# Where layer 1's results lie before they are stored: first five images in place, runs of eight rows from the sixth on

## The chip, the core and the metric

The kernel runs on one core of one Trainium2 chip. The metric is device time in microseconds for one launch; three runs of the kernel before took 1414.7 to 1417.7 us, with a median of 1415.74 us. A smaller time is better.

## What is computed

The input `x` holds 16 images of 128 channels and 64 x 64 pixels in float32. Two layers are applied, each with a residual:

```
x = x + L0(groupnorm(x))     # diagonal LSTM: a scan over 64 + 63 skewed columns
x = x + L1(groupnorm(x))     # per pixel: 128 channels -> 4 angles -> 4-qubit circuit -> 128 channels
```

Layer 1 works on each pixel alone. With the normalisation folded into its weights, it is for each pixel: angles (a product with 4 rows of weights, expanded to 128 rows of signed sums), a sine, a product to amplitudes, a square, a product back to 128 channels, a bias, and the residual. Groups of four channels share their mean and variance over an image, so layer 1 can only start once layer 0 has finished every row of every image.

## The kernel before

**Where the data lies.** A tile called `ring` holds 40 of the 64 rows of all 16 images in on-chip memory, as `[128 channels, 10 blocks, 16 images, 256]`; a block is four rows of one image, 1 KB per channel, and the blocks of one image are 16 KB apart. The other 24 rows, the "low" rows, go out to a scratch tensor `low` in device memory while layer 0 runs, and must be loaded again for layer 1.

**Layer 1's tiling.** A chunk is eight rows of one image: 512 values, 2 KB, for each of the 128 channels. An image has eight chunks, k = 0 to 7. Chunks 0 to 2 are low rows (`NT` is 3); chunks 3 to 7 lie in the ring, as two neighbouring blocks, so in two pieces of 1 KB. For each image `angles` (L977) makes the angles of all eight chunks, `sines` (L992 to L997) reduces them and takes the sine, `squares` (L1006, L1019) the amplitudes and their squares, `outputs` (L1028) the products for half of the chunks, h = 0 or 1, four PSUM banks at a time out of five, and `finish` (L1053, L1054) adds bias and residual on VectorE and has SP store each chunk to `out`. Image 0 is done in two half-width passes (c = 0 and 1); the others in one (c is None).

**Where results go.** `finish` writes the result of a low chunk where the chunk was (`v`). For images 1 to 15 the result of a ring chunk goes somewhere else: for an odd image b to `ring[:, q, b-1:b+1]`, for an even one to `ring[:, q+1, b-2:b]`. These are blocks of the image itself and its neighbours that are dead by then, and as images are neighbours in memory, the 512 values are one run of 2 KB. Image 0 is written in place.

**Places for low rows.** There are 48 low chunks. `lows` lists where each of them lies, in the order of images. The first 14 places are the eight `spare` tiles and six `low` tiles; the first eight are filled during layer 0, by SP. Each `finish` appends the places that it has used to the list `places`, in order, and `load(n)` takes up to n of them from its front and has POOL load the next low chunks into them (L860). A load must wait until the store that reads its place has landed. In image 0 only the low chunks' places are appended (`c == 1 and k < NT`); from image 1 on all eight.

**What sets the order.** The stage is written under a manual schedule: each engine and queue runs its instructions in the order of the program and waits on semaphores only. In layer 1 SP's queue holds nothing but the stores, POOL's nothing but the loads. VectorE runs, for image b, four additions, the rounding of image b + 2 (L994, L995), and four more additions. The loop over b calls `outputs`, `finish(b, 0)`, `load(3)`, the sine, `squares(b + 1)`, `outputs`, `finish(b, 1)`, `load(3)`, `angles(b + 3)`.

Of the kernel before, what the change touches and what calls it, by code (L numbers as in the profile page):

```python
# [25 lines left out]
BLOCK = ROWS * NW  # L26
# [54 lines left out]
def kernel(  # L81
# [16 lines left out]
    nc = tc.nc  # L98
# [12 lines left out]
    NT = NLOW * NW // CHUNK  # L111
# [23 lines left out]
    def block(r):  # L135

        return (r + AHEAD if r < SLOTS else r - SLOTS) // ROWS
# [18 lines left out]
    with ExitStack() as scan:  # L156
# [58 lines left out]
        with ExitStack() as prep:  # L215
# [47 lines left out]
            for i in range(2):  # L263
                nc.scalar.dma_start(out=ws_n[i], in_=ws_v[:, 2 * i : 2 * i + 2])
            nc.scalar.dma_start(
                out=qw, in_=q_weights.rearrange("l w a -> (l w a)").partition_broadcast(P)
# [88 lines left out]
            for i in range(2):  # L355
                v = ws_n[i]
# [500 lines left out]
        def low_rows(queue, n, v):  # L857
            b, k = n // NT, n % NT
            of = low[b, :, k * CHUNK : (k + 1) * CHUNK]
            queue.dma_start(out=v, in_=of if len(v.shape) == 2 else of.rearrange("p (k n) -> p k n", n=BLOCK))  # L860
# [4 lines left out]
        with tc.manual_schedule():  # L865
# [26 lines left out]
            v = ring[:, block(NH - ROWS)].rearrange("p i (r w) -> p i r w", w=NW)[:, :, :, NW - STRIP :]  # L892
# [4 lines left out]
            for i, u in enumerate((d, sq)):  # L897
                u = u.rearrange("p i r w -> p i (r w)")
# [43 lines left out]

    places = list(spare) + [lowp.tile([P, CHUNK], F32, name=f"low{i}") for i in range(6)]
    lows = []

    def load(n):

        while n and places and len(lows) < NT * NB:  # L950
            v = places.pop(0)
            lows.append(v)
            if len(lows) > 8:
                low_rows(nc.gpsimd, len(lows) - 1, v)
            n -= 1

    def rows_of(b, k):
        if k < NT:
            return lows[NT * b + k]
        q = block(2 * ROWS * k)  # L960
        return ring[:, q : q + 2, b, :]

    def half(v, c):

        if c is None:
            return v
        return v[:, c] if len(v.shape) == 3 else v[:, c * BLOCK : (c + 1) * BLOCK]

    def bank(pool, name):
        return pool.tile([P, CHUNK], F32, name=name, tag=pool.name)  # L970

    def angles(b, c=None, all_of=None):
        th = half(bank(ps_t, f"theta{b}_{c}") if all_of is None else all_of, c)
        for h in range(2):

            for j in (2, 3, 1, 0):
                nc.tensor.matmul(  # L977
                    th[32 * j : 32 * j + 32, :],
                    lhsT=w_image[:, b, 16 - 16 * h : 48 - 16 * h],
                    rhs=half(rows_of(b, 2 * j + h), c),  # L980
                    start=(h == 0),
                    stop=(h == 1),
                    tile_position=(0, 32 * j),
                )
        ths[b, c] = th

    def sines(b, c=None):

        if b not in turns:
            turns[b] = sinp.tile([P, CHUNK], F32, name=f"y{b}", tag="y")  # L990
        y = half(turns[b], c)
        nc.scalar.activation(y, ths[b, c], AF.Identity, bias=b_image[:, b : b + 1])  # L992
        near = half(nearp.tile([P, CHUNK], F32, name=f"near{b}_{c}", tag="near"), c)
        nc.vector.tensor_scalar(near, y, ROUND, ROUND, ALU.add, ALU.subtract)  # L994
        nc.vector.tensor_sub(y, y, near)  # L995
        yield
        nc.scalar.activation(y, y, AF.Sin, scale=TWO_PI)  # L997

    def squares(b, c=None):
        ams = []  # L1000
        y = half(turns[b], c)
        for h in range(2):
            am = half(ps_a.tile([P, CHUNK], F32, name=f"am{b}_{h}_{c}", tag=f"am{h}"), c)

            k = 64 * h
            nc.tensor.matmul(  # L1006
                am,
                lhsT=w_amp[k : k + 64, h, :],
                rhs=y[k : k + 64, :],
                start=True,  # L1010
                stop=True,
                tile_position=(k, 0),
            )
            ams.append(am)

        if b not in sqs:
            sqs[b] = [sqp.tile([P, CHUNK], F32, name=f"sq{b}", tag="sq"), turns[b]]
        for am, v in zip(ams, sqs[b]):
            nc.scalar.activation(half(v, c), am, AF.Square)  # L1019

    def outputs(b, h, c=None):
        po = [
            half(bank(ps_o, f"po{b}_{h}_{j}_{c}"), c)
            for j in range(4)
        ]
        for j in range(4):
            k = 32 * j
            nc.tensor.matmul(  # L1028
                po[j],
                lhsT=w_out[k : k + 32, :],  # L1030
                rhs=half(sqs[b][h], c)[k : k + 32, :],
                start=True,
                stop=True,
                tile_position=(k, 0),
            )
        return po

    def finish(b, h, po, c=None):
        for j in range(4):
            k = 4 * h + j  # L1040
            v = rows_of(b, k)
            x1, y, o = half(v, c), po[j], ov[b, :, k * CHUNK : (k + 1) * CHUNK]
            to = place = v
            if c is not None:
                o, to = o[:, c * BLOCK : (c + 1) * BLOCK], x1
            elif k >= NT:


                q = block(2 * ROWS * k)
                to = ring[:, q, b - 1 : b + 1, :] if b % 2 else ring[:, q + 1, b - 2 : b, :]  # L1050
                y = y.rearrange("p (k n) -> p k n", n=BLOCK)
                place = to.rearrange("p k n -> p (k n)")
            nc.vector.scalar_tensor_tensor(to, y, b_out, x1, ALU.add, ALU.add)  # L1053
            nc.sync.dma_start(out=o, in_=to if c is not None else place)  # L1054
            if c is None or c == 1 and k < NT:
                places.append(place)

    def idle():

        ps = bank(ps_t, nc.get_next_instruction_name())  # L1060
        v = w_image.rearrange("p b k -> p (b k)")[:, 0:CHUNK]
        for _ in range(2):
            nc.tensor.matmul(ps, lhsT=w_out, rhs=v, start=True, stop=True)  # L1063

    with tc.manual_schedule():
        load(len(places))

        angles(0, 0)
        angles(0, 1, bank(ps_o, "theta0"))
        first = [sines(0, c) for c in range(2)]  # L1070
        for later in first:
            next(later)

        th = bank(ps_t, "theta1")
        angles(1, 0, th)
        for later in first:
            next(later, None)
        squares(0, 0)
        angles(1, 1, th)
        ths[1, None] = th  # L1080
        po = outputs(0, 0, 0)
        finish(0, 0, po, 0)
        squares(0, 1)
        later = sines(1)
        next(later)
        po = outputs(0, 1, 0)
        finish(0, 1, po, 0)
        next(later, None)
        po = outputs(0, 0, 1)
        finish(0, 0, po, 1)  # L1090
        load(3)
        angles(2)
        later = sines(2)
        next(later)
        po = outputs(0, 1, 1)
        squares(1)
        next(later, None)
        finish(0, 1, po, 1)
        angles(3)
        for b in range(1, NB):  # L1100
            po = outputs(b, 0)
            later = sines(b + 2) if b + 2 < NB else iter(())
            finish(b, 0, po)
            load(3)
            next(later, None)
            if b + 1 < NB:
                squares(b + 1)
            next(later, None)
            po = outputs(b, 1)
            finish(b, 1, po)  # L1110
            load(3)
            if b + 3 < NB:
                angles(b + 3)
            elif b < NB - 1:
                idle()
# [37 lines left out]
```

## Time and profile before

| what | value |
|---|---|
| median of three runs | 1415.74 us |
| the profiled execution's own time | 1416.6 us |
| its span, first to last instruction | 1414.8 us |
| granted TensorE clock over the span | 0.994 |
| busy share over the span: TensorE, VectorE, ScalarE, GpSimd | 96%, 69%, 55%, 65% |
| moved in all | 107.06 MB |
| stores of results from the ring, 256 KB each | 94, median 5.1 us from issue to landing |
| loads of low rows by POOL's queue | 40 of 256 KB |
| one addition L1053, 128 x 512 | 743 ns, 94 into the ring, 14 into spare tiles, 12 into low tiles |

The span is one execution, taken by the hardware profiler; the 1.8 us between it and that execution's time lie before the first and after the last instruction. Layer 1 is the last 130 us or so. The busy shares of the whole span say little about it: they are means over the scan of layer 0, which TensorE fills, and over layer 1. "Landing" is the moment at which the transfer's completion arrives; a transfer's time from issue to landing contains its time in the queue behind others. Instructions that overlap in an engine's pipeline have durations (743 ns) longer than their pace.

### The profile page before, as it was taken

To read this page: it belongs to the slowest core of one execution; us is meant where nothing else is said; L and a number is where in the kernel's file an instruction comes from. 1 tells how busy PE (TensorE), PEld (TensorE's weight loads), DVE (VectorE), ACT (ScalarE), POOL (GpSimd) and SP (SyncE) were. 2 spreads that over 40 slices of the span, in tenths; PEclk is the share of its full clock that TensorE was granted. 3 is DMA by queue.
4 is the path that set the end of the run, shared out by engine and by line. 5 is a ranking of instruction groups with operands and counts; after the bars stand their busy time and mean duration, and the time that the engine had idled before them with its cause. 6 is when DMAs were issued, how large, how long until landed. Compare 5 with 4: busy or idle time off the path is not lost. (4 is left out here: it accounts for less than half of the span.)

```text
span 1414.8 us, 20302 instructions
## 1 busy us (share of the span) xinstructions
PE 1351.9 (96%) x6030; PEld 960.6 (68%) x6030; DVE 981.1 (69%) x2549; ACT 778.4 (55%) x1860; POOL 921.3 (65%) x1823
## 2 busy tenths in 40 slices
PE   6778999999999999999999999999999999989995
PEld 5658887777776667667777767677777778785331
DVE  7983565566665666787777776666665567866995
ACT  4555666555555555555555555555555566554331
POOL 4226787777776667788888876777777667762300
PEclk9999999999999999999999999999999999999998
DMA  9980000000000000133333100000000000004999
GB/s 327 368 282 2 1 2 0 1 1 1 1 0 1 0 1 1 60 119 120 119 120 120 60 1 1 0 1 1 1 1 0 1 1 1 9 24 157 371 399 353
DMA packets 78926, 107.06 MB, mean 76 GB/s; under 512 B 5552, under 2 KB 53712, under 8 KB 78816
## 3 DMA queue, kind: packets, MB, share of 16 engines
q1 hardware_dynamic: 74176, 94.39, 19.1%
q0 software_dynamic: 3408, 10.58, 2.1%
q8 instruction: 48, 0.79, 0.2%
q10 hardware_dynamic: 1232, 0.80, 0.2%
q14 instruction: 62, 0.51, 0.1%
HBM read 59.61 MB, written 46.14 MB: 75 GB/s over the span
## 5 line engine op out<-in xcount | busy, mean ns | idle before, releaser
L583 PE MATMUL ps<-spare,wxT 128*128 128x512 f32 (+18 forms) x1280 | 479.7, 518 | 0.7 <-POOL spare L574 0.7
L767 DVE TENSOR_TENSOR ps<-ps,both 128x256 f32<-128x256 f32 (+9 forms) x544 | 221.7, 408 | 304.9 <-PE ps L752 303.4
L771 ACT ACTIVATE ps<-ps,bias 128x512 f32<-128x512 f32 (+23 forms) x480 | 279.3, 583 | 220.2 <-DVE ps L767 183.7
L752 PE MATMUL ps<-spare,w1T 128*128 128x256 f32 (+16 forms) x1272 | 345.8, 353 | 9.8 <-DVE spare L834 4.9
L583 PEld LDWEIGHTS ps<-spare,wxT 128*128 128x128 f32 x1280 | 230.9, 190 | 173.2 <-issue 155.5
L752 PE MATMUL ps<-spare,w0T 128*128 128x256 f32 (+16 forms) x1272 | 343.8, 352 | 0.8 <-POOL spare L608 0.8
L802 ACT COPY both<-ps 128x256 f32<-128x256 f32 (+9 forms) x544 | 191.6, 355 | 180.8 <-PE ps L752 161.2
L617 POOL TENSOR_TENSOR ring<-ring,spare 128x256 f32<-128x256 f32 (+8 forms) x487 | 247.7, 541 | 31.2 <-DVE stats L705 21.1
L752 PEld LDWEIGHTS ps<-spare,w1T 128*128 128x128 f32 x1272 | 229.8, 190 | 35.7 <-DVE spare L834 7.6
L752 PEld LDWEIGHTS ps<-spare,wsT 128*128 128x128 f32 x1088 | 194.9, 190 | 86.4 <-DVE spare L834 34.7
L752 PE MATMUL ps<-spare,wsT 128*128 128x256 f32 (+14 forms) x1088 | 241.3, 365 | 5.4 <-DVE spare L834 3.6
L752 PEld LDWEIGHTS ps<-spare,w0T 128*128 128x128 f32 x1272 | 230.3, 190 | 22.1 <-POOL spare L608 0.9
L574 POOL TENSOR_TENSOR spare<-spare,rstd 128x512 f32<-128x512 f32 (+10 forms) x160 | 171.1, 1069 | 14.8 <-DVE rstd L153 2.3
L569 POOL TENSOR_TENSOR spare<-ring 128x256 f32<-128x256 f32 (+8 forms) x213 | 147.6, 703 | 0.0
L828 ACT ACTIVATE g<-cst 128x256 f32<-128x256 f32 (+20 forms) x320 | 103.0, 368 | 64.4 <-DVE cst L827 63.8
L564 POOL TENSOR_TENSOR spare<-ring,mean 128x16 f32<-128x16 f32 (+8 forms) x247 | 131.2, 541 | 7.4 <-DVE mean L143 7.2
L834 DVE TENSOR_TENSOR spare<-g,ps 128x256 f32<-128x256 f32 (+17 forms) x319 | 105.4, 368 | 43.9 <-ACT g L828 42.0
L608 POOL TENSOR_TENSOR spare<-spare 128x240 f32<-128x240 f32 (+9 forms) x136 | 102.7, 755 | 29.6 <-DVE spare L834 25.7
L771 ACT ACTIVATE g<-ps,bias 128x512 f32<-128x512 f32 (+20 forms) x160 | 97.4, 609 | 27.1 <-DVE ps L767 21.1
L827 DVE TENSOR_TENSOR cst<-cst,ps 128x256 f32<-128x256 f32 (+20 forms) x320 | 104.5, 368 | 5.5
L854 POOL COPY spare<-spare 128x16 f32<-128x16 f32 x64 | 21.1, 330 | 133.8 <-DVE spare L834 133.8
L824 DVE TENSOR_TENSOR ps<-ps,g 128x512 f32<-128x512 f32 (+20 forms) x160 | 95.1, 594 | 17.0 <-ACT g L771 16.6
(368 smaller groups left out, 1096.6 us busy)
## 6 DMA issues: line engine op xcount, KB each, us to landing
out_dram<-ring SPq DMA_DIRECT2D x94, 256.0 KB, 5.1
ring<-in_x_dram SPq DMA_DIRECT2D x80, 256.0 KB, 5.6
low<-ring SPq DMA_DIRECT2D x6, 2048.0 KB, 7.5
ring<-in_x_dram SPq DMA_DIRECT2D x6, 2048.0 KB, 8.1
spare<-in_x_dram SPq DMA_DIRECT2D x27, 256.0 KB, 5.5
rest<-in_x_dram SPq DMA_DIRECT2D x21, 256.0 KB, 5.6
ring<-low POOLq DMA_DIRECT2D x19, 256.0 KB, 6.3
out_dram<-spare SPq DMA_DIRECT2D x14, 256.0 KB, 6.5
```

What stands on the lines that cost most here:

```text
L564: nc.gpsimd.tensor_sub(by_pairs(xn, 0, j, n), x0, over(mean1, n))
L569: nc.gpsimd.tensor_sub(by_pairs(xn, 1, j, n), lower, of)
L574: nc.gpsimd.tensor_mul(v, v, r)
L583: nc.tensor.matmul(ps[g][:, :, a:b], lhsT=wxT[:, g * 128 : (g + 1) * 128], rhs=xns[t % 2][:, :, a:b], start=t > 0, stop=True, skip_group_c ...
L617: engine.tensor_add(x1, x1, by_pairs(new, q, j, n))
L752: nc.tensor.matmul(out, lhsT=w[:, g * 128 : (g + 1) * 128], rhs=rhs, start=False, stop=True, skip_group_check=True,)
L767: nc.vector.tensor_add(v, v, both[g][:, a:b])
L771: nc.scalar.activation(to[:, :, a:w], ps[g][:, :, a:w], FUNC[g], bias=bias[:, g : g + 1])
L802: nc.scalar.copy(both[g][:, a:b], ps[g][:, 0, a:b])
L827: nc.vector.tensor_add(c[:, q], c[:, q], ig[:, q])
L828: nc.scalar.activation(th[:, q, a:w], c[:, q], AF.Tanh)
L834: nc.vector.tensor_mul(new[:, q, a:v], th[:, q, a:v], act[GO][:, q, a:v])
```

## The change

A constant `RUNS = 5` is added, and images are told apart by it.

- Images 5 to 15 put the results of their ring chunks into runs of 2 KB, as before. Images 1 to 4 put them in place (`v`), like image 0: two pieces of 1 KB, and the store to `out` has the shape 128 x 2 x 256.
- Image 0's ring chunks now hand their places on too (with c = 1), as do those of images 1 to 3: places of two pieces. Image 4's ring chunks hand none on, since image 5's and image 6's runs go there; images 5 and later do as before. The number of places handed on is enough for all 48 low chunks. The five of image 0 stand early in the line.
- A low chunk can therefore lie in a place of two pieces, and is then loaded, used and stored in that shape.
- `load(2)` is called once more, after image 0; in the loop the second `load(3)` of an image becomes `load(2)`.

```diff
+    RUNS = 5
     places = list(spare) + [lowp.tile([P, CHUNK], F32, name=f"low{i}") for i in range(6)]
...
             to = place = v
             if c is not None:
                 o, to = o[:, c * BLOCK : (c + 1) * BLOCK], x1
-            elif k >= NT:
+            elif k >= NT and b >= RUNS:
                 q = block(2 * ROWS * k)
                 to = ring[:, q, b - 1 : b + 1, :] if b % 2 else ring[:, q + 1, b - 2 : b, :]
                 y = y.rearrange("p (k n) -> p k n", n=BLOCK)
                 place = to.rearrange("p k n -> p (k n)")
+            elif k >= NT:
+                y, o = (u.rearrange("p (k n) -> p k n", n=BLOCK) for u in (y, o))
             nc.vector.scalar_tensor_tensor(to, y, b_out, x1, ALU.add, ALU.add)
-            nc.sync.dma_start(out=o, in_=to if c is not None else place)
-            if c is None or c == 1 and k < NT:
+            nc.sync.dma_start(out=o, in_=to if place is v else place)
+            if c != 0 and (k < NT or b != RUNS - 1):
                 places.append(place)
...
         finish(0, 1, po, 1)
+        load(2)
         angles(3)
...
             finish(b, 1, po)
-            load(3)
+            load(2)
```

## The prediction

> **What bounds the kernel now.** The change touches only the last stage (layer 1), so I read, in this order: the granted clock (0.994, so nothing is throttled for long), the windows table of the last 130 us, the chain that ended last, and the timelines of VectorE and of SP's queue.
>
> Windows of the kernel before (columns: window, its length, busy us and instruction count of PE, PEld, DVE, ACT, POOL, then the TensorE clock, the DMA share and GB/s):
>
> ```profile
> 1300.00:1308.00 8.00, 8.00 (x56) 1.96 (x48) 3.70 (x9) 2.98 (x5) 1.61 (x3) 0.84 0.74 245
> 1308.00:1316.00 8.00, 8.00 (x45) 2.85 (x44) 7.97 (x14) 3.04 (x6) 2.35 (x5) 1.00 0.79 243
> 1324.00:1332.00 8.00, 8.00 (x53) 2.59 (x46) 7.97 (x13) 3.33 (x6) 3.23 (x6) 1.00 1.02 403
> 1340.00:1348.00 8.00, 8.00 (x48) 2.63 (x44) 7.97 (x14) 3.40 (x6) 3.22 (x6) 1.00 1.04 411
> 1388.00:1396.00 8.00, 8.00 (x35) 2.92 (x34) 7.20 (x12) 1.09 (x2) 0.00 (x0) 1.00 1.03 383
> 1404.00:1412.00 8.00, 0.00 (x0) 0.00 (x0) 0.00 (x0) 0.00 (x0) 0.00 (x0) 0.50 1.00 375
> ```
>
> Two resources are full. VectorE is busy 7.97 of every 8 us from 1308 on: one image costs 6.33 us (eight additions of L1053 at a 0.66 us pace, plus rounding). The DMA engines are full from about 1316 to 1412, eleven microseconds after the last compute. The chain shows where compute stops, and what a cold TensorE costs (the same 16 matmuls, 3.55 against 1.85 us):
>
> ```profile
> 1299.14 3.55 PE theta_None L977 x16
> 1304.39 1.85 PE theta_None L977 x16
> ...
> 1399.90 1.32 DVE ring L1053 x2
> ```
>
> So VectorE ends at 1401.2, and the stores it left behind end the kernel: the last is issued at 1409.4, takes 4.2 us to land (1413.6), and 1.2 us of closing semaphores make 1414.8. Today stores late by 10 us hold nobody up. How late they are is seen at image 4. VectorE (first column the start):
>
> ```profile
> 1328.30 0.74 DVE L1053 SCALAR_TENSOR_TENSOR ring<-po_None,b_out,ring 128x512 f32<-128x512 f32 x1
> ...
> 1330.02 2.72 DVE L1053 SCALAR_TENSOR_TENSOR ring<-po_None,b_out,ring 128x512 f32<-128x512 f32 x4
> ...
> 1334.64 0.74 DVE L1053 SCALAR_TENSOR_TENSOR ring<-po_None,b_out,ring 128x512 f32<-128x512 f32 x1
> ...
> 1336.35 2.72 DVE L1053 SCALAR_TENSOR_TENSOR ring<-po_None,b_out,ring 128x512 f32<-128x512 f32 x4
> ```
>
> The first two rows are image 4's chunks k=3 and k=4 to 7, the last two image 5's. SP's queue issues image 4's five ring stores here:
>
> ```profile
> 1336.39 5.46 SPq L1054 DMA_DIRECT2D out_dram<-ring  x5
> ```
>
> The first of them (issued 1336.4) and the last (1341.5) then land after
>
> ```profile
> DMA to landing us min/median/max: 10.1/10.1/10.1
> ...
> DMA to landing us min/median/max: 9.4/9.4/9.4
> ```
>
> that is at 1346.5 and 1350.9, when VectorE has long finished image 5 (1336.35 + 2.72 = 1339.1).
>
> **What the Trainium skill says.** "TensorE: Matmul & The Clock Gate", Architectural detail: VectorE's queue is strict first in, first out, so one waiting addition holds all behind it; the timeline's unchanging order fits. The same page, Part 1 (the HAM clock gate): after an idle window of some 3.4 us TensorE runs at half clock until as long a busy one; the 3.55 against 1.85 us above agrees. "DMA: Bandwidth & Descriptors", Queues, rings and completion order: each DMA engine takes turns between queues packet by packet; from 1324 to 1356 POOL's queue moved 6.66 MB and SP's 6.37 MB, so loads do take half from the stores. The same page, Why small descriptors are slow: a fixed cost per packet. The trace shows it between layer 0's 1 KB stores of low rows (587 to 591, 347 GB/s) and the 2 KB stores of the tail (1404 to 1410, 381 GB/s):
>
> ```profile
> DMA packets 1356, 1.39 MB, mean 347 GB/s; under 512 B 0, under 2 KB 1356, under 8 KB 1356
> ...
> DMA packets 1258, 2.29 MB, mean 381 GB/s; under 512 B 144, under 2 KB 144, under 8 KB 1257
> ```
>
> **The change, part by part.**
>
> 1. *Images 1 to 4 stay in place.* The additions keep shape and count: 0 us on VectorE. Removed are waits of images 1 and 2 on image 0's stores; those had landed about 2 us after issue and stopped VectorE nowhere (1309.97 on it never idles): 0.
>
> 2. *Smaller packets.* 20 stores of images 1 to 4, and later 20 stores of low rows that lie in two-piece places, go in 1 KB pieces. One costs 262,144 B / 347 = 0.755 against 0.688 us, 0.07 more; the small completion packets (144 in one window, 0 in the other) hide part of it, and if they cost up to a 1 KB packet each it is 0.13. I take 0.10: 40 x 0.10 = 4 us of DMA time. The 20 loads into such places have no row: from 0 (POOL's packets stay 4 KB: 3200 for 40 loads, 80 each, 16 of them completions) to 0.12 each like the stores; I take 0.05, 1 us in all. More pieces for POOL to describe may lengthen its 0.54 us per load, covered since POOL does nothing else.
>
> 3. *Loads start sooner.* Image 0's five ring places now take low rows. From 1300 to 1316 only 3.90 MB moved where 408 GB/s (the rate of 1324 to 1356) gives 6.5 MB, so five more loads (1.31 MB) fit: 1.31 / 0.408 = 3.2 us of DMA work pulled into idle time. Every later load takes a place five further back in the line, so the 40 are all issued before image 4's ring stores have landed; before, 36 had landed by 1351. Two loads after an image's second half instead of three do not slow this: POOL runs ahead until a place's store has landed.
>
> 4. *A new wait.* From image 5 on, results go to runs as before, and image 5's run at `ring[:, q, 4:6]` overlaps image 4's own block, which now still holds image 4's result until its store has landed. In the changed program's instruction order image 5's additions k=3 to 7 wait for exactly those five stores. The work behind them in VectorE's queue is everything: image 7's rounding, all later images; TensorE then waits for PSUM banks, SP for results.
>
> When do they land? Last one before: 1350.9. By then four more loads have moved (4 x 0.643 = +2.6), five fill idle time (-3.2), some 15 saturated 1 KB stores (+1.5), some 18 ring loads (+0.9): 1352.7. Image 5's last addition ends 0.7 later, 1353.4, against 1339.1: **a stall of 14.3 us**. During it the DMA works off its backlog, so afterwards VectorE alone sets the pace (8 stores need 8 x 0.69 = 5.5 of 6.33 us). VectorE ends at 1401.2 + 14.3 = 1415.5; the last store starts 0.2 later and lands in 2.5 to 3 us (2.4 to 2.6 from 1308 to 1312, when the queue was short); 1.2 us close: 1419.6. TensorE idles some 8 us in the stall and starts cold: at half clock its 5 us per image become 10 against 6.33 for perhaps 4 us, less the five filled PSUM banks; 0 to 1.5 us, I take 0.6. Sum: 1420.2 for the span, +5.4. The profiled execution itself took 1416.6 us (1.8 around the span); the median of the runs is 1415.74, so the forecast is 1415.74 + 5.4 = **1421.1 us**.
>
> **Rivals.** *A, the stores get ahead (not slower).* Break-even is where 1401.2 + stall + 0.2 + 2.5 reaches the old landing of 1413.6: a stall of 9.7 us, image 4's last store landing at 1348.3. If five loads fewer stand in front of image 4's stores and 1 KB costs nothing, it lands at 1350.9 - 3.2 = 1347.7; VectorE then ends before the DMA, which gains 3.2 us: 1415.7 - 3.2 = 1412.5. Against it: the loads released sooner fill what they empty. *B, DMA still sets the end.* Stall under 9.7 us but packets paid: 4 + 1 - 3.2 = +1.8, up to 5.2 + 2.4 - 3.2 = +4.4: 1417.5 to 1420, middle 1418. *C, the stall is longer.* 1 KB stores take a smaller turn against 4 KB load packets and ring loads cost 0.12: landing at 1355 to 1357, cold TensorE 1.5: 1424.5. *D, the wait does nothing*, because the stores land before image 5: they would have to land by 1334.6, though SP issued them from 1336.4 on; 1 in 50, included in A.
>
> **How the numbers follow.** Forecast 0.62 (its own range 1419 to 1423), C 0.16, B 0.13, A 0.09. A change counts from 0.2%, 2.8 us, about what a measurement of this kernel can tell from none: 1412.9 to 1418.6. Faster: most of A, 0.06. Same: the rest of A and two thirds of B, 0.11. Slower: 0.83. Leaving out A and the low end of B, and the far end of C, the range is 1416.8 to 1425.5.
>
> **What would show it.** VectorE idle of 12 to 16 us between about 1335 and 1353, released by stores from the ring at image 5's k=3 to 7, and nowhere else; VectorE's end near 1415; SP afterwards issuing each store within a microsecond of its addition; DMA below full from about 1360. Five POOL loads into the ring before 1311 show part 3; the rate of the stores of images 1 to 4 shows part 2. I am wrong if image 4's stores land by 1348, or if the backlog remains after image 5.

## The result and the profile after

The changed kernel takes 1424.69 us (median of four runs, 1423.03 to 1425.56); the kernel before, run on the same chip, has a median of 1416.49 us in four runs. The ratio is 1.0064, with a 95% interval of 1.0051 to 1.0076: slower by 8 to 9 us (the medians lie 8.2 us apart), as forecast in direction, larger than forecast in size (1421.1 us, range 1416.8 to 1425.5). A few executions of `hold` and `RUNS = 3`, among them the first that was profiled of `RUNS = 3`, ran at a lower granted clock (0.56 to 0.94) and took 1459 to 2334 us; medians and ratios leave them out.

The profiled execution took 1423.03 us, with a span of 1421.2 us against 1414.8 us. It was the shortest of the four; the spans of the others were 1422.4, 1423.4 and 1423.7 us. In the changed kernel `finish` issues its additions at L1056 and its stores at L1057.

Windows of the kernel after (columns as before: window, length, busy us and count of PE, PEld, DVE, ACT, POOL, TensorE clock, DMA share, GB/s):

```profile
1300.00:1308.00 8.00, 8.00 (x54) 2.15 (x48) 4.02 (x9) 3.23 (x6) 2.32 (x4) 0.89 0.78 256
1308.00:1316.00 8.00, 8.00 (x44) 2.66 (x40) 7.96 (x14) 3.23 (x6) 4.37 (x7) 1.00 0.91 303
...
1340.00:1348.00 8.00, 0.08 (x1) 0.11 (x1) 0.97 (x2) 0.00 (x0) 3.25 (x5) 0.50 1.06 403
1348.00:1356.00 8.00, 8.00 (x16) 2.80 (x20) 6.29 (x11) 1.51 (x3) 0.00 (x0) 0.50 1.05 403
1356.00:1364.00 8.00, 8.00 (x43) 2.12 (x40) 6.07 (x10) 3.18 (x6) 0.00 (x0) 0.77 0.81 296
1388.00:1396.00 8.00, 8.00 (x48) 2.63 (x44) 7.96 (x14) 3.40 (x6) 0.00 (x0) 1.00 0.85 302
1404.00:1412.00 8.00, 8.00 (x34) 2.73 (x33) 7.41 (x12) 1.17 (x3) 0.00 (x0) 1.00 0.96 342
```

Before, VectorE was busy 7.93 to 7.97 us in each window from 1308 to 1364, and the DMA engines were full until 1412 while compute had ended at 1401. Now TensorE, VectorE and ScalarE all but stand still from 1340 to 1348 with the DMA full (1.06); from 1356 on the DMA has room (0.81, 0.85) and VectorE is what is full. The bound has changed over from the stores to VectorE.

VectorE's timeline of the kernel after, around image 5 (start, duration, what, count; in brackets the idle time ahead of it and its releaser):

```profile
1333.36 0.74 DVE L1056 SCALAR_TENSOR_TENSOR ring<-po_None,b_out,ring 128x512 f32<-128x512 f32 x1
1347.03 0.75 DVE L1056 SCALAR_TENSOR_TENSOR ring<-po_None,b_out,ring 128x512 f32<-128x512 f32 x1 [12.93 <-DMA out_dram<-ring]
...
1350.11 1.41 DVE L1056 SCALAR_TENSOR_TENSOR ring<-po_None,b_out,ring 128x512 f32<-128x512 f32 x2 [0.62 <-DMA out_dram<-ring]
1352.59 3.38 DVE L1056 SCALAR_TENSOR_TENSOR ring<-po_None,b_out,ring 128x512 f32<-128x512 f32 x5 [1.06 <-DMA out_dram<-ring]
...
1357.70 2.73 DVE L1056 SCALAR_TENSOR_TENSOR ring<-po_None,b_out,ring 128x512 f32<-128x512 f32 x4 [0.67 <-PE po_None L1029]
```

The second row is image 5's k = 3. It waits 12.93 us for a store out of the ring; two of the chunks behind it wait another 0.62 and 1.06 us. The last row waits for a product, not for a store. SP's queue of the kernel after issued the stores in question, image 4's, here:

```profile
1336.38 7.46 SPq L1057 DMA_DIRECT2D out_dram<-ring  x5
```

The one issued at 1336.38 landed 10.6 us later, at 1346.9, where VectorE starts again; the last, issued at 1343.5, landed at 1352.5, where the last of the waits ends. The addition of the first had started at 1327.69: its store spent 8 us in the program's queue before its issue, and then as long again and more on the way.

The list of waits from 1302 to the end, first of the kernel after (engine, line, what it waited for: us in total, times, longest), then of the kernel before:

```profile
DVE ring L1056 <- DMA out_dram<-ring: 14.6, 3, 12.9
DVE ring L1056 <- PE po_None L1029: 2.7, 3, 1.2
```

```profile
DVE ring L1053 <- PE po_None L1028: 0.8, 1, 0.8
```

So there are 14.6 us of new waits for stores, and 1.9 us of new waits for TensorE (2.7 less the 0.8 that was there). The chain that ended last, of the kernel after, shows both together (start, duration, what):

```profile
1326.85 9.46 DMA out_dram<-ring
...
1336.38 10.56 DMA out_dram<-ring
...
1347.03 0.76 DVE ring L1056
...
1347.92 5.73 PE po_None L1029 x8
1353.65 2.01 PE am_None L1007 x4
1355.66 2.02 PE po_None L1029 x8
1357.68 2.89 PE theta_None L978 x16
1360.57 1.07 PE po_None L1029 x8
1361.64 1.06 PE am_None L1007 x4
...
1364.90 1.85 PE theta_None L978 x16
```

Two stores in a row carry the chain for 20 us: the second, image 4's first, was issued when the first, one of image 3's, had landed. Then comes TensorE at half clock (2.89 us for the angles of an image, which take 1.85 us later; the trace has two records for each product of the program, so x16 are eight products), and from there on compute to the end. The last store is issued at 1417.6, lands in 2.4 us, and the span ends 3.6 us after VectorE, where it was 13.6 us before.

One pair of numbers is used below for every kernel: the time from image 1's first addition to the end of VectorE (93.9 us before, 1307.33 to 1401.22; 110.9 us after, 1306.67 to 1417.57) and the tail from there to the end of the span. The new delay of VectorE is 17.0 us, of which the waits named make 16.5. The other 0.5 us is about what five interruptions cost: an addition that starts after a gap takes its full 0.74 us, where one in a row adds 0.66 us (an estimate, 5 x 0.08 = 0.4 us).

### The profile page after: what moved, and what is told of

It is laid out like the page before. It is cut to its first block, busy times and chain, and to the rows that moved or that the text cites. A ratio compares the mean times of both kernels' runs of the same rounds, so it can differ in the third digit from the quotient of the medians.

```text
span 1421.2 us, 20299 instructions
## 1 busy us (share of the span) xinstructions
PE 1357.7 (96%) x6030; PEld 962.7 (68%) x6030; DVE 981.1 (69%) x2549; ACT 777.8 (55%) x1860; POOL 923.4 (65%) x1823
```

## The experiments

The theory at this point is that of the prediction: image 5's additions wait for image 4's stores; this delays VectorE by more than the 10.0 us (13.6 less 3.6) by which the stores used to end later, so VectorE sets the end. The rivals: that the sooner loads make the stall (they stand in front of the stores), that the smaller pieces make the loss, and that cold TensorE is what was sized wrong.

The profiles of all kernels, from their VectorE timelines and lists of waits (us; waits for TensorE without the 0.8 us near the end that every kernel has, and counted from image 1's first addition on; in `after_again` and `runs4` one wait is moved from TensorE to the stores, for the reason given under `after_again`):

| kernel | image 1's first addition | to VectorE's end | waits for stores | waits for TensorE | tail | span |
|---|---|---|---|---|---|---|
| before | 1307.3 | 93.9 | 0 | 0 | 13.6 | 1414.8 |
| after | 1306.7 | 110.9 | 14.6 | 1.9 | 3.6 | 1421.2 |
| after_again | 1307.7 | 112.0 | 15.1 | 2.7 | 3.7 | 1423.4 |
| hold | 1306.5 | 94.0 | 0 | 0 | 14.1 | 1414.6 |
| inplace_only | 1304.8 | 110.9 | 13.8 | 2.7 | 3.5 | 1419.2 |
| runs7 | 1305.0 | 111.6 | 14.5 | 3.0 | 3.7 | 1420.3 |
| runs4 | 1308.0 | 105.8 | 9.5 | 1.7 | 3.6 | 1417.3 |
| runs3_again | 1307.7 | 104.0 | 6.5 | 3.0 | 3.5 | 1415.2 |
| all_in_place | 1308.3 | 93.9 | 0 | 0 | 17.5 | 1419.6 |
| hold_late | 1307.9 | 94.6 | 0 | 0.6 | 14.5 | 1417.0 |
| warm | 1309.0 | 117.2 | 14.2 | 8.4 | 4.4 | 1430.5 |
| warm11 | 1306.7 | 111.5 | 15.0 | 1.9 | 3.7 | 1421.8 |
| hold3 | 1309.1 | 93.9 | 0 | 0 | 12.2 | 1415.2 |

### after_again: the changed kernel once more

No edit. The kernel before, run beside it, had a median of 1416.53 us.

> The changed kernel once more, beside the edits below. Theory (image 5 waits for image 4's stores, then TensorE is cold): the same as before, 1423 to 1426 us, VectorE idle 14 to 17 us in all between the third addition of image 5 and the first of image 6; the length of that idle time alone should follow the spread of 2.5 us between runs of this kernel. Rival (something outside layer 1 drifts from run to run): layer 1 takes the same time and the start of layer 1 moves.

Measured: 1424.53 us (1421.79 to 1425.14), ratio 1.0059 [1.0042, 1.0076]. VectorE's timeline of this profile at image 5 (the first row is its k = 3, the last begins with its k = 6), and TensorE's of image 5's second half:

```profile
1348.61 0.75 DVE L1056 SCALAR_TENSOR_TENSOR ring<-po_None,b_out,ring 128x512 f32<-128x512 f32 x1 [13.56 <-DMA out_dram<-ring]
...
1353.27 4.04 DVE L1056 SCALAR_TENSOR_TENSOR ring<-po_None,b_out,ring 128x512 f32<-128x512 f32 x6 [1.53 <-PE po_None L1029]
```

```profile
1334.58 1.64 PE L1029 MATMUL po_None<-y,w_out 32*128 32x512 f32 x8
```

The profile puts the 1.53 us down to TensorE, but the product for image 5's k = 6 was done by 1336.2. By the program, what was left to wait for is image 4's store of k = 6, for which the trace has no landing. So the waits for stores are 13.56 + 1.53 = 15.1 us, and those for TensorE 1.81 + 0.87 = 2.7 us, against 14.6 and 1.9 us in the first profile. The wait for stores lies in the 14 to 17 us that I expected, but it isn't what the two executions differ by: of 2.2 us of span, 0.5 come from it, 0.8 from TensorE and 1.0 from a later image 1, which was the rival.

### hold: the wait taken away, the rest of the change kept

Image 5's five ring results go to five spare tiles, which images 1 and 2 don't hand on; the pairs of blocks of later runs are shifted by one image.

```diff
+    hold = spare[3:8]
...
-                to = ring[:, q, b - 1 : b + 1, :] if b % 2 else ring[:, q + 1, b - 2 : b, :]
-                y = y.rearrange("p (k n) -> p k n", n=BLOCK)
-                place = to.rearrange("p k n -> p (k n)")
+                if b == RUNS:
+                    to = place = hold[k - NT]
+                else:
+                    d = (b - RUNS) % 2
+                    to = ring[:, q, b - 1 : b + 1, :] if d else ring[:, q + 1, b - 2 : b, :]
+                    y = y.rearrange("p (k n) -> p k n", n=BLOCK)
+                    place = to.rearrange("p k n -> p (k n)")
...
+            kept = k < NT and 3 <= NT * b + k < 8
-            if c != 0 and (k < NT or b != RUNS - 1):
+            if c != 0 and not kept and (k < NT or b != RUNS - 1):
```

> Image 5's five ring results go to five spare tiles that images 1 and 2 don't hand on, and the later runs pair images (5,6), (7,8), ... so that no run touches image 4's blocks; all else of the change stays (in place, two-piece places, image 0's places for loads). Theory (the wait on image 4's stores is the whole loss): VectorE never idles over 1 us at image 5, ends near 1401, the stores' backlog sets the end again, 1413 to 1417 us. Rival (1 KB pieces or the sooner loads cost most of the 8 us): still 1420 us or more.

Measured: 1416.3 us, ratio 1.0003 [0.9994, 1.0013]. VectorE's timeline of this kernel at image 5 (its k = 3 and k = 4 to 7):

```profile
1333.92 0.74 DVE L1061 SCALAR_TENSOR_TENSOR spare<-po_None,b_out,ring 128x512 f32<-128x512 f32 x1
...
1335.64 2.72 DVE L1061 SCALAR_TENSOR_TENSOR spare<-po_None,b_out,ring 128x512 f32<-128x512 f32 x4
```

There is no gap, although SP issued image 4's stores in the same place as in the changed kernel (from 1336.0). VectorE ends 94.0 us after image 1's first addition, and stores end the kernel again, 14.1 us later. The whole loss hangs on whether image 5's results and the runs behind them go where image 4's stores still read. The small pieces and the sooner loads, which this kernel keeps, cost nothing together that can be measured.

### inplace_only: images 1 to 4 in place, without the sooner loads

```diff
-            if c != 0 and (k < NT or b != RUNS - 1):
+            if c is None and (k < NT or b != RUNS - 1) or c == 1 and k < NT:
...
-        load(2)
...
-            load(2)
+            load(3)
```

> Images 1 to 4 in place and runs from image 5 on, but image 0 hands on its low places only and the loads are called as before (three and three). Theory (the wait comes from where the results lie, not from the loads): a stall of 12 to 16 us at image 5, 1421 to 1425 us. Rival (the sooner loads delay image 4's stores and so make the stall): image 4's stores land about 4 us sooner than in the changed kernel and the time is 1416 to 1420 us.

Measured: 1422.08 us (1420.96 to 1423.44), ratio 1.0049 [1.003, 1.0067]. The list of waits of this kernel:

```profile
DVE ring L1056 <- DMA out_dram<-ring: 13.8, 3, 11.2
DVE ring L1056 <- PE po_None L1029: 2.7, 2, 1.8
```

The stall is there without the sooner loads, so they don't make it. The rival had one thing right: the last of the waits ends at 1349.2 in place of 1352.6; but as image 5 comes 1.9 us earlier as well, the wait is only 0.8 to 1.3 us shorter. Its span is 2.0 us below that of the changed kernel; 1.9 of these come from an earlier image 1 (1304.8 against 1306.7).

### runs3, runs4 and runs7: the same wait against a smaller and a larger backlog

```diff
-    RUNS = 5
+    RUNS = 3
```

and the same with 7. For 4 the pairs of blocks are shifted as well: `if (b - RUNS) % 2 == 0` in place of `if b % 2`. The wait then falls on image 3, 4 or 7.

> The change with RUNS = 3: the new wait falls on image 3, at about 1321 us, when the stores are only 7 to 9 us from issue to landing. Theory (loss = stall beyond the 9.7 us by which the stores lagged behind VectorE at the end): a stall of 4 to 7 us, below that margin, so the DMA sets the end: 1412 to 1417 us. Rival (any such stall costs its length, or the in-place images cost by their number): 1419 us or more.

> The change with RUNS = 7: the new wait falls on image 7, whose stores of image 6 are then 13 us late by the profile before (image 6's spare stores were issued 13 us after their addition) and take 6 us to land. Theory: a stall of 12 to 16 us and a cold TensorE, 1421 to 1426 us. Rival (after the last load the backlog drains, so a later image waits less): a stall under 10 us, 1416 to 1419 us.

> Changed kernel with runs from the fifth image on instead of the sixth (the pairs of blocks shifted by one, so that each run takes the same blocks relative to its image). The new wait then meets the stores of image 3, for which the backlog is smaller: with RUNS = 3 VectorE waited 4.3 us on stores, with 5 14.6 us, so some 9 us here, plus 2 to 3 us on a cold TensorE. The forecast's break-even is 9.7 us of total delay. If that balance is right, VectorE ends within 3 us of the point at which it sets the end: ratio 1.000 to 1.003 (1416 to 1420 us), between RUNS = 3 and RUNS = 5. Rival: the loss is a fixed price of smaller packets or of the later runs, not of the length of the stall; then the ratio is that of RUNS = 5 and 7, 1.005 to 1.006.

> RUNS = 3 once more, for an undisturbed profile. VectorE's waits on stores at image 3 3 to 5 us, on TensorE 1 to 3 us, VectorE's end 1405 to 1409, and the span's end still set by stores that were queued, with a tail of 6 to 10 us between VectorE's last addition and the end of the span and DMA at 1.0 to the end. Span 1414 to 1417. Rival (the stall sets the end whatever its length): a tail of 3.5 to 4 us and a span of 1418 or more.

Measured: RUNS = 3, 1415.8 us, ratio 0.9999 [0.999, 1.0008]; RUNS = 4, 1419.03 us, ratio 1.0023 [1.0015, 1.0032]; RUNS = 7, 1423.44 us, ratio 1.0052 [1.0037, 1.0067]. The rows of VectorE's waits for stores in the lists of waits, first of RUNS = 3 (second profile), then of RUNS = 4, then of RUNS = 7:

```profile
DVE ring L1056 <- DMA out_dram<-ring: 6.5, 3, 5.4
```

```profile
DVE ring L1056 <- DMA out_dram<-ring: 8.9, 4, 7.8
```

```profile
DVE ring L1056 <- DMA out_dram<-ring: 14.5, 1, 14.5
```

With the 0.56 us that `RUNS = 4` has ahead of image 4's k = 6, these are 6.5, 9.5 and 14.5 us, and 14.6 with RUNS = 5. The later the image that has to wait, the longer the stall, up to image 5; at image 7 it is as long, so the rival, a backlog that drains after the last load, is out for these images. The balance can be read off: RUNS = 4 delays VectorE by 105.8 - 93.9 = 11.9 us, 1.9 more than the 10.0 that the old tail of stores hid, and image 1 started 0.6 us later: 2.5 us, which is what the span shows (1417.3 against 1414.8). RUNS = 3 delays it by 10.1 us, just what was hidden, and costs 0.4 us of span in the one execution that this profile shows. What I expected of its second profile was still wrong: the tail was to be 6 to 10 us, set by queued stores. It was 3.5 us, as in the kernels that VectorE bounds; I had gone by the 4.3 us of waits for stores that the first profile lists, and here they are 6.5 (another 1.49 us there, ahead of image 3's k = 6, stands under TensorE). A stall of this length is free only just.

### all_in_place: no runs at all

```diff
-    RUNS = 5
+    RUNS = 16
```

Nothing waits, and every ring result is stored in 1 KB pieces.

> RUNS = 16: every image in place, so no run and no such wait, but all 75 ring stores of images 1 to 15 and all stores from two-piece places go in 1 KB pieces. Theory (a 1 KB store costs 0.10 us more of DMA time and the DMA sets the end): some 55 more such stores than in hold, 1416.4 + 5.5 = 1420 to 1424 us, with 347 GB/s or a little more at the end. Rival (the pieces cost 0.02 to 0.03 us or nothing, as the 400 against 407 GB/s in the mixed phase suggests): 1416 to 1418.5 us.

Measured: 1420.46 us (1419.06 to 1421.75), ratio 1.0032 [1.002, 1.0044]. VectorE has no new gap (93.9 us); the stores end the kernel 17.5 us after it. The tail's window of this kernel, and of the kernel before:

```profile
1372.00:1404.00 32.00, 28.04 (x129) 9.43 (x128) 29.25 (x46) 7.61 (x13) 0.00 (x0) 0.94 1.02 347
```

```profile
1372.00:1404.00 32.00, 27.10 (x126) 9.13 (x124) 28.32 (x45) 7.61 (x13) 0.00 (x0) 0.96 1.02 382
```

Both are full (1.02), at 347 and 382 GB/s: 0.755 and 0.686 us for each 262,144 B. The 55 ring stores of images 5 to 15 that `hold` makes in runs at 380 GB/s (0.690 us) and this kernel in pieces then cost 55 x 0.065 = 3.6 us; the two ratios differ by 0.0029, 4.1 us. The price of a small piece was right for a phase of stores alone. Beside loads it is smaller: from 1324 to 1346 this kernel moves 403 GB/s and the kernel before 407, with 4.7 and 4.6 MB of it loads.

### hold_late: without the wait, without the sooner loads

`hold` with the edits of `inplace_only` to the places and loads.

```diff
-            if c != 0 and not kept and (k < NT or b != RUNS - 1):
+            if (c is None and not kept and (k < NT or b != RUNS - 1)) or (c == 1 and k < NT):
...
-        load(2)
...
-            load(2)
+            load(3)
```

> hold, but image 0 hands on its low places only and the loads are called as before: without the sooner loads. Theory of the prediction (five loads fill idle DMA time worth 3.2 us, which the 1 KB pieces of hold give back): 1418.5 to 1420.5 us. Rival (the sooner loads bring nothing, they only take the place of stores that then come later): the same as hold within 1 us, 1415.5 to 1417.5 us.

Measured: 1417.46 us, ratio 1.0014 [1.0005, 1.0022]; `hold` had 1.0003 [0.9994, 1.0013]. Where stores set the end, the sooner loads are thus worth some 0.0011, about 1.6 us, half of the 3.2 us that I had given them, and as the intervals overlap it isn't shown that they are worth anything. The time lies below what the theory expected and just within what the rival did (1415.5 to 1417.5 us). The comparison isn't quite of the loads alone, since image 0's five two-piece places drop out with them.

### warm and warm11: TensorE kept busy through the stall

Eleven dummy products of 128 x 512 behind image 8's angles, into a bank that is written anew afterwards; `warm` has one more after each of image 6's first four outputs.

```diff
+    def warm_pe(n):
+        am = ps_a.tile([P, CHUNK], F32, name=nc.get_next_instruction_name(), tag="am0")
+        v = w_image.rearrange("p b k -> p (b k)")[:, 0:CHUNK]
+        for _ in range(n):
+            nc.tensor.matmul(am, lhsT=w_out, rhs=v, start=True, stop=True)
...
+            if b == RUNS + 1 and h == 0:
+                warm_pe(1)
...
+                if b == RUNS:
+                    warm_pe(11)
```

`warm11` leaves out the `if b == RUNS + 1` lines.

> The changed kernel with dummy products on TensorE while it waits in the stall: eleven of 128 x 512 after image 8's angles, one after each of image 6's first four outputs, into a PSUM bank that nobody reads then. Theory (TensorE comes cold out of the stall and costs 2 to 4 us on top of the wait): VectorE's waits on TensorE between images 5 and 7 fall from 2 to 4 us to under 1 us, 1421 to 1423 us. Rival (the stores' landing alone sets the resumption): 1424 to 1426 us, or longer where the dummies run on.

> Changed kernel with eleven dummy products of 128x512 behind the angles of image 8, and none between image 6's products. They fill the stretch in which TensorE waits for image 5's additions, and do not compete with useful products after it. If cold TensorE after the stall is the part of the loss that the forecast sized too small, VectorE's waits on TensorE at images 6 and 7 fall from 1.9 to 4.2 us to under 0.5 us and the time falls by that much, to 1421 to 1423 us (ratio 1.003 to 1.0045). Rival: the thin products of 32 rows after the stall let the clock fall whatever came before; then the waits on TensorE stay at 1.5 to 4 us and the time at 1424 to 1425 (ratio 1.0055 to 1.0065).

Measured: `warm` 1434.49 us (1432.28 to 1436.35), ratio 1.0135 [1.0118, 1.0153]; `warm11` 1423.65 us, ratio 1.0052 [1.0037, 1.0067], for which the changed kernel has 1.0064 and 1.0059. Neither is the gain that the theory expected; `warm11` lies between what the theory and the rival gave, and its waits for TensorE speak for the rival. Windows of `warm11`:

```profile
1346.00:1348.00 2.00, 0.82 (x2) 0.00 (x0) 0.70 (x2) 0.00 (x0) 0.55 (x1) 1.00 1.09 404
1348.00:1350.00 2.00, 1.29 (x3) 0.47 (x4) 1.81 (x5) 0.86 (x2) 0.00 (x0) 0.82 1.04 400
1350.00:1352.00 2.00, 2.00 (x4) 0.82 (x4) 0.68 (x1) 0.35 (x1) 0.00 (x0) 0.50 1.05 416
...
1358.00:1360.00 2.00, 2.00 (x16) 0.32 (x12) 0.92 (x2) 0.67 (x2) 0.00 (x0) 0.62 0.66 244
1360.00:1362.00 2.00, 2.00 (x20) 0.54 (x12) 1.80 (x3) 0.69 (x1) 0.00 (x0) 1.00 0.68 255
```

The dummies end at 1346.8 with the clock at full, as they were meant to. It falls within 1348 to 1350 all the same, while image 5's additions free banks two or so at a time and TensorE has only 3 or 4 records, two to a product, in 2 us, and comes back at about 1359, as in the changed kernel. VectorE's waits for TensorE are again 1.9 us. In `warm` the clock stayed up until 1353, but the extra products ran into the half-clock phase, where one takes 2.0 us in place of 1.05; VectorE waited 8.4 us for TensorE. So the cold phase isn't set by the idle 10 us alone: the thin flow behind it is enough. Its price could only be read from the waits; no run has TensorE at full clock through that stretch, so that half clock makes the waits is argued and not shown. An estimate from the chain of the kernel after speaks for it: from 1353.65 on, three blocks of products that stand ahead of those for image 7's additions took 2.01 + 2.02 + 2.89 = 6.9 us, and blocks of the same kinds take 1.06 + 1.07 + 1.85 = 4.0 us soon after; the 2.9 us between them are more than the 1.9 us that VectorE waited.

### hold3: what the runs point to

`hold` with `RUNS = 3`: no wait, and ten stores fewer in small pieces.

```diff
-    RUNS = 5
+    RUNS = 3
```

> The variant that takes image 5's results to free places instead of the ring, but with runs from the fourth image on (RUNS = 3), so that only images 1 and 2 are stored in 1 KB pieces. Theory: no wait for a store at image 3, because the five free places were emptied by low-row stores of images 1 and 2, some 5 us before the ring stores that stopped RUNS = 3 for 6.5 us; the DMA's backlog sets the end, ten stores fewer in small pieces than with RUNS = 5 (10 x 0.07 = 0.7 us of DMA time) and the five sooner loads kept: 1415 to 1416.5 us, ratio 0.999 to 1.0005. Rival: those five places aren't free in time, VectorE waits 1 to 4 us at image 3 (which the tail of stores still covers), and one load comes later for want of a place: ratio 1.000 to 1.002.

Measured: 1415.97 us (1414.19 to 1417.34), ratio 0.9999 [0.999, 1.0007]. VectorE's timeline of this kernel at image 3 (the first row is its k = 3, the next its k = 4 to 7):

```profile
1323.72 0.74 DVE L1061 SCALAR_TENSOR_TENSOR spare<-po_None,b_out,ring 128x512 f32<-128x512 f32 x1
...
1325.43 2.72 DVE L1061 SCALAR_TENSOR_TENSOR spare<-po_None,b_out,ring 128x512 f32<-128x512 f32 x4
```

There is no gap here either. The kernel is even with the kernel before, and nothing that was run beats it by what can be measured.

## Why the prediction was right in kind and short in size

**Part 1 (in place, 0 us): right.** `hold` and `all_in_place` keep it, and VectorE takes 94.0 and 93.9 us from image 1 on, as before (93.9). (That VectorE never idles from 1309.97 on isn't quite so: it waits 0.76 us for a product at 1395, as it does near the end in the other kernels.)

**Part 2 (smaller pieces, 4 us and 1 us of DMA time): right per store where stores are alone, too much beside loads.** 347 against 382 GB/s in the tail, but 400 against 407 GB/s from 1324 to 1346 in the changed kernel. The 7 GB/s over 22 us are 0.4 us, where the forecast of the landing had 1.5 + 0.9 = 2.4 us for stores and loads together. A load into two pieces took POOL 0.70 to 0.73 us to issue, up from 0.54, and hid as said.

**Part 3 (five sooner loads, -3.2 us): the loads came as said, their worth was half or less.** POOL's timeline of the kernel after:

```profile
1302.80 0.73 POOL L860 DMA_DIRECT2D ring<-low  x1
1308.09 2.14 POOL L860 DMA_DIRECT2D ring<-low  x3 [4.55 <-DVE spare L1056]
1310.71 0.70 POOL L860 DMA_DIRECT2D ring<-low  x1 [0.48 <-DVE y L996]
```

These are five loads into the ring before 1311. From 1300 to 1316 the kernel moved 4.47 MB against 3.90 MB, 0.57 MB more, which at 408 GB/s is 1.4 us; I had put the full 1.31 MB there. The second profile of the same kernel moved only 3.95 MB, and `inplace_only`, without these loads, 4.52 MB: how early image 1 starts counts as much as what may be loaded, and the 1.4 us can't be put down to the loads alone.

**Part 4, the wait: right in place, cause and length.** It was to be 14.3 us, with the last landing at 1352.7; it is 14.6 us, at 1352.5, and 15.1 us in the second profile. `hold` shows that it is the cause, and RUNS = 3 and 4 show the break-even: 9.7 us in the prediction, 10.0 us measured. The length is right partly by luck, since in it, as far as the windows above tell, two errors cancel: loads -1.4 in place of -3.2, pieces +0.4 in place of +2.4.

**Part 4, what follows the wait: this step failed.** "TensorE idles some 8 us in the stall and starts cold ... 0 to 1.5 us, I take 0.6." VectorE waited 1.9 us for TensorE in the first profile and 2.7 us in the second; in `inplace_only` and RUNS = 7, 2.7 and 3.0. I had counted 4 us of half clock, from the stall's end. The clock was at 0.50 from 1339.3 to 1359.7, so for 12.7 us after the stall's end at 1347.0, and for seven after VectorE's last wait for a store: the phase in which image 5's banks come free one by one left TensorE cold. In addition 0.3 to 0.5 us of VectorE's delay is in no wait that the profile lists.

The sum for the profiled execution, by the prediction's terms: wait +0.3, TensorE +1.3, unlisted +0.5, tail 3.6 in place of 4.1 us -0.5, image 1 earlier -0.7: +0.9 on the forecast +5.4, and the span grew by 6.4. For the second: +0.8, +2.1, +0.3, -0.4, image 1 later +0.3: +3.1, and the span grew by 8.6. The median, 8.2 us up, lies near the second.

**The rivals.** A and D are out: the stores landed at 1352.5, not by 1348. B's condition, a stall under 9.7 us, isn't met here; `hold` comes nearest to it, with no stall, stores at the end, and the pieces and sooner loads of the change: +0.0003 (-0.0006 to +0.0013), 0.4 us and at most B's +1.8. (The landing that goes with a stall of 9.7 us is 1348.1 by the prediction's own sum, not 1348.3.) C has the number nearest to the median (1424.5) but not by its mechanism: of its two parts, the landing at 1355 to 1357 didn't happen, and the waits for TensorE were more than its 1.5 us.

**What would show it.** VectorE's gap at image 5 was there, but not "nowhere else": images 6 and 7 had the waits for TensorE. VectorE's end was to be near 1415 and was 1417.6. The DMA below full from about 1360 is there (0.81 from 1356 to 1364).

**What stays open.** Whether half clock alone makes the waits for TensorE, and why they vary from 1.9 to 2.7 us in one kernel. Image 1's first addition falls anywhere from 1304.8 to 1309.1, and the traces show a large part of the reason: just ahead of it TensorE is at half clock for no time at all (`hold`, `inplace_only`, `runs7`, `warm11`), for 3.4 us (before, after) or for 6.8 us (the others). VectorE's waits there, for ScalarE and then for TensorE, are 1.5 + 1.1 us in the first case, 3.1 + 1.1 us in the second and 3.7 + 1.6 to 2.1 us in the third; this makes up the 1.0 us between the two profiles of the changed kernel (1306.7 and 1307.7). What decides between the three isn't known. A kernel that VectorE bounds shows such a shift in full.

## What to carry to other kernels

Before letting a result go where a store still reads, read from the profile when that store lands, not when it is issued: a queue that is late without harm becomes a stall as soon as somebody waits for it. Such a stall, with what comes behind it, costs what exceeds the slack at the end (here 10.0 us). Price what comes behind, the restart of the engines that starved, until they run dense work again, not until the wait ends. Where a profile names an engine as the cause of a wait, look whether that engine had long been done. If the wait can't be had earlier, five free places at that one point are enough to take it away.

## What was not expected of the hardware

- TensorE's stretches at half clock in layer 1, but for the last, which the end cuts off, lasted 3.4, 6.8, 10.2, 13.7, 17.1 or 20.5 us, always a multiple of 3.4 us (20.5 us in the changed kernel, from 1339.3 to 1359.7; 10.2 us in `warm11`, from 1349.3 to 1359.5). "TensorE: Matmul & The Clock Gate", Part 1 (the HAM clock gate), says that the gate watches how busy the array was in a free-running window of some 3.4 us, which fits. Its table gives half clock after an idle window; here the clock fell 2.1 us after the last product in the changed kernel, and 2.4 us after the last dummy in `warm11`, while a few products still ran, so a window need not be wholly idle. How much work counts as busy no run here shows.
- 1 KB pieces lowered the rate by 9% where only stores ran (347 against 382 GB/s) and by 1 to 2% where loads ran beside them (400 and 403 against 407 GB/s; in `hold_late`, where loads were less of the traffic, 3.47 of 8.53 MB in place of 4.56 of 8.95, 388 GB/s).
- A 256 KB load into two-piece places cost POOL 0.70 to 0.73 us to issue, against 0.54 us into places of one run.
